# Two layers' query and key block products dealt out in one written order, and a tail with its projection and additions rearranged

## The chip, the cores and the metric

The kernel runs on one core of a Trainium2 chip. The metric is the device time of one execution in microseconds (us); lower is better. The time before is 3595.53 us, the median of three runs (3595.47 to 3596.08). One more execution was recorded by the hardware profiler; its own numbers are in the table below.

A core has five engines that run side by side and wait for each other through semaphores: TensorE (PE; PEld is its loading of weights), VectorE (DVE), ScalarE (ACT), GpSimd (POOL) and SyncE (SP), which mostly issues transfers. Matmul results land in PSUM, in banks of 512 fp32 values per partition, and VectorE or ScalarE take them out.

## The reference, cut to what matters

The input is 16 images of 256 channels and 1024 positions. Each goes through two layers, all in fp32. Both layers compute queries, keys and values from the tokens:

```python
# layer 0, 4 heads of 64
qkv = (xs @ w_proj + b_proj).reshape(B, S, N_HEADS, 3 * D_K)
q, k, v = jnp.split(qkv, 3, axis=-1)
attn = jax.nn.softmax(jnp.einsum('bihd,bjhd->bijh', q, k) * SCALE, axis=2)
res = jnp.einsum('bijh,bjhd->bihd', attn, v).reshape(B, S, N_HEADS * D_K)
x = res @ w_out + b_out + xs
# layer 1, 8 heads of 32
x = x + attention(group_norm(x, gn1_w, gn1_b), qkv_w, proj_w, proj_b, phys_bias)
h = gelu(mlp_w1 @ group_norm(x, gn2_w, gn2_b) + mlp_b1, approximate=False)
out = x + mlp_w2 @ h + mlp_b2
```

The change concerns `q` and `k` of both layers, the order of some sums around them, and, for the last image alone, the projection of layer 1 (`res @ proj_w`) and the additions of the second MLP matmul to the output.

## The kernel before, in words

The images run through a software pipeline. While image b is in attention, pieces of the MLP of image b-1 and of the `v` of image b+1 are put between its steps. For images 1 to 14 (14 times in all) there is a stage between layer 0's attention and layer 1's attention of image b. It holds, on TensorE, the first half of the previous image's MLP (`hidden`, line 1206), then `q` and `k` of layer 0 for image b+1 and of layer 1 for image b (line 1103), then layer 1's scores (line 642).

There `q` and `k` are not made by eight block products for each half of the output channels but by seven. Four blocks of the input (two halves of the channels by two halves of the positions) and four of the weights are combined beforehand: the input sums `t1` to `t4` by four VectorE instructions (`input_sums`, lines 1088 to 1091), the weight sums once, at the beginning. Then `qk_by_seven` issues products p1 to p7 for each of two channel halves `ch`. All products of a half gather in three PSUM banks: two banks of one "wide" tile (`both`), and one bank `y`. Between products, ScalarE copies a state of a bank aside (`qk7p`, lines 1128 to 1136) or out as `k` (lines 1109, 1111), and VectorE takes out `q` (lines 1115, 1117). A later product into the same tile has to wait for such a reader.

In what follows a product is named by layer, number and half: "a20" is product 2 of half 0 for layer 0 (image b+1), "b31" product 3 of half 1 for layer 1 (image b).

What decides the order of the work: the program issues pieces in a written order, but instructions without a marker can be moved by the building layer's scheduler, which gives every engine one fixed order before the run. `keep_in_program_order` takes an instruction out of that freedom, and `issue_after(x)` keeps what stands in its block behind the instruction x. On the chip each engine then works through its own list in order; at the head of a list an instruction waits for its semaphores.

In the kernel before, the products have no marker. The build puts p7 of half 1 of layer 0 (a71) into the MLP's first half, and mixes the others. The layer-1 input sums are made as soon as the group norm's four `gn_g` instructions (line 928) are done. On VectorE they stand ahead of the last GELU sums of the MLP's first half (lines 1262, 1263 and 1282; the first two read MLP products from PSUM, and the third waits for ScalarE's GELU, line 1221). The `v` product of layer 1's first positions comes in the middle of the block products.

The tail belongs to the last image. From the end of its second attention on, a list `nc.in_order` is set, and every instruction of VectorE and TensorE issued through it keeps the written order; such instructions carry the helper's line, L64. The projection `j` of a position half (`out_proj`, `issue`) runs, for each output half, over both input halves; the second input half waits for VectorE's scaling of `res_b`. Six additions of the previous image's MLP result to the output (`add_up`, line 1343, `x<-x,lent`) are held in the list `put_off` together with the sums for a range check, and are all issued within the first pieces of the last image's MLP (`begin`).

Of the kernel before, what the change touches and what calls it, by code (L numbers as in the profile page):

```python
# [283 lines left out]
def first_pass(ctx, tc, x, out, k):  # L284
# [55 lines left out]
    def bank(name, n):  # L340
        return ps_a.tile([P, TB], F32, tag=f"b{n}", name=name)
# [273 lines left out]
    def attention_b(b, qT, kT, v, project):  # L615
# [134 lines left out]
        def normalise(i, r, last):  # L750
            t, c = items[i]
            at_end = last and b == B - 1
            den = bank(f"den_{key}_{i}", 1)
            for g in range(G):
                nc.tensor.matmul(
                    den[g * D : (g + 1) * D, :],
                    k["eones"][:, c * G + g],
                    sums[i][:, g, :],
                    start=True,
                    stop=True,  # L760
                )
            full = work.tile([P, TB], F32, tag="full", name=f"rd_{key}_{i}", bufs=2)
            if at_end:

                held = work.tile([P, TB], F32, tag="full", name="den_held", bufs=2)
                nc.scalar.copy(held, den)
                nc.vector.reciprocal(full, den)
                scale(i, r, last, full)
                put_off.append(lambda: add_to_range(held, full))
                return  # L770
            denominators(
                f"{key}_{i}", den, full, full,
                (3, 5) if last else (1, 1),
                lambda full: scale(i, r, last, full),
            )
# [33 lines left out]
    def out_proj(key, w, src, bias, xs, t, stats, then, late=False):  # L809
        todo = list(range(CC))  # L810

        def issue(cos=range(CC), apart=False):
            home = None if apart else spare.pop("home", None)
            apart = apart or cols[0] == P
            if not apart:
                both = wide(f"{key}_{t}")
            ps = {}

            def leave(co, held=None):
                y = xs[:, co, t * TB : (t + 1) * TB]  # L820
                nc.vector.scalar_tensor_tensor(
                    y, ps[co] if held is None else held[:, co], bias[:, co : co + 1], y,
                    ALU.add, ALU.add,
                )
                nc.vector.bn_stats(stats[:, co, t, :], y)
                if held is None:
                    todo.remove(co)

            def add_up(held):
                with tc.issue_after(spread_out["es"].ins):  # L830
                    for co in range(CC):
                        leave(co, held)

            def part(co, kc):
                product(
                    ps[co],
                    w[:, kc, co * P : (co + 1) * P],
                    src(kc),
                    start=(kc == 0),
                    stop=(kc == CC - 1),  # L840
                )

            for co in cos:
                ps[co] = bank(f"{key}_{t}_{co}", co) if apart else both[:, co, :]
            if apart:
                for co in cos:
                    for kc in range(CC):
                        part(co, kc)
                    leave(co)
            else:  # L850
                for kc in range(CC):
                    for co in cos:
                        part(co, kc)
                if home is not None:
                    held = home[:, 2:4]
                    nc.scalar.copy(held, both)
                    later.after(1, lambda: add_up(held))
                elif late:
                    later.after(2, lambda: [leave(co) for co in cos])
                else:  # L860
                    for co in cos:
                        leave(co)
            if not todo and then:
                then()

        return issue
# [227 lines left out]
    made_k = []  # L1094

    def qk_by_seven(key, block, s, x, q, kk, bias=None):
        ps, got = {}, []

        def half(d, ch, t):
            return d[:, ch, t * TB : (t + 1) * TB]  # L1100

        def mm(to, w, right, first):
            nc.tensor.matmul(  # L1103
                to, w, x[right], start=first, stop=True, skip_group_check=not first
            )

        def leave_k(to, what, ch):
            if bias is None:
                made_k.append(nc.scalar.copy(to, what))
            else:  # L1110
                nc.scalar.activation(to, what, AF.Identity, bias=bias[:, 1, ch : ch + 1])

        def leave_q(to, what, more, ch):
            if bias is None:
                nc.vector.tensor_add(to, more, what)
            else:
                nc.vector.scalar_tensor_tensor(
                    to, what, bias[:, 0, ch : ch + 1], more, ALU.add, ALU.add
                )

        def p1(ch):
            both = wide(f"qk7_{key}_{ch}")
            ps[ch] = both[:, 0, :], both[:, 1, :], bank(f"qk7y_{key}_{ch}", 1 - ch)
            if not got:
                got.append(weights_tile(f"qk7p_{key}"))
            one, two, _ = ps[ch]
            mm(one, block(1, ch, 0), "b11", True)
            nc.scalar.copy(two, one)

        def p7(ch):  # L1130
            mm(ps[ch][2], s[:, ch, 2], "t3", True)
            nc.scalar.copy(got[0][:, 2 * ch], ps[ch][2])

        def p6(ch):
            mm(ps[ch][1], s[:, ch, 1], "t2", False)
            nc.scalar.copy(got[0][:, 2 * ch + 1], ps[ch][1])

        def p2(ch):
            mm(ps[ch][0], block(1, ch, 1), "b21", False)
            leave_k(half(kk, ch, 0), ps[ch][0], ch)  # L1140

        def p4(ch):
            mm(ps[ch][2], block(0, ch, 1), "t4", False)
            leave_q(half(q, ch, 0), ps[ch][2], got[0][:, 2 * ch + 1], ch)

        def p5(ch):
            mm(ps[ch][1], s[:, ch, 0], "t1", False)
            leave_q(half(q, ch, 1), ps[ch][1], got[0][:, 2 * ch], ch)

        def p3(ch):  # L1150
            mm(ps[ch][1], s[:, ch, 3], "b22", False)
            leave_k(half(kk, ch, 1), ps[ch][1], ch)

        return [
            lambda p=p, ch=ch: p(ch)
            for p, ch in (
                (p1, 0), (p1, 1), (p7, 0), (p7, 1), (p6, 0), (p6, 1), (p2, 0),
                (p5, 0), (p5, 1), (p4, 0), (p4, 1), (p2, 1), (p3, 0), (p3, 1),
            )
        ]  # L1160

    inputs = {}

    put_off = []

    def sums_of_input(b, y, part=None):
        extra = act.tile([P, 3, TB], F32, tag="hs", name=f"hs_{b}")
# [26 lines left out]
    def mlp(b, xb):  # L1194
# [30 lines left out]
        def begin(i):  # L1225
# [14 lines left out]

            if not nc.in_order:
                return add_once()
            put_off.insert(i, add_once)
            if i:
                while put_off:
                    put_off.pop(0)()
                nc.in_order.clear()

        def middle(i):
# [6 lines left out]
        def finish(i):  # L1256
# [3 lines left out]
            products_of(i, [(7, ps[:, 0, :], False), (6, ps[:, 1, :], False)])  # L1260
            rest = gs[1, 1, i]
            nc.vector.tensor_add(unit(0, 0, i), rest, ps[:, 0, :])  # L1262
            nc.vector.tensor_add(rest, rest, ps[:, 1, :])
            gelu(0, 0, i, gs[0, 0, i])
            gelu(1, 1, i, rest)
            combine((1, 0), (0, 0), False, i)
# [195 lines left out]
    for b in range(B):  # L1462
        def load_next(b=b):
# [3 lines left out]
            with tc.issue_after(spread_out["last"].ins):  # L1467
                load_blocks(1, b - 1)
                if b + 1 < B:
# [2 lines left out]
        later.after(14, load_next)  # L1472
        xn = []
        seven = 0 < b < B - 1
        sums_1 = {}
        run(
            attention_0(
                b, tiles0, xs[b],
                lambda st, b=b, xn=xn, seven=seven, sums_1=sums_1: group_norm(
                    f"g{b}", xs[b], st, k["g1w"], k["g1b"], "res", xn, 2 if b else 1,  # L1480
                    (lambda y: sums_1.update(input_sums(f"b{b}", y))) if seven else None,
                ),
            )
        )
# [4 lines left out]
        if seven:  # L1489
# [2 lines left out]
            run_pieces(hidden[1:2])  # L1492
            with tc.issue_after(mlp_made["begun"].ins):
                sums_0 = input_sums(f"a{b}", xs[b + 1])
            run_pieces(hidden[2:])
            first = first_v
            run_pieces(
                qk_by_seven(
                    f"a{b}", qk_block_0, qk_parts[:, 0], sums_0, *tiles0[:2], k["bqk"]
                )  # L1500
            )
        else:
            run_pieces(first[:5] if b == 0 else hidden)
        later.flush()
# [7 lines left out]


        if seven:
            made = qk_by_seven(f"b{b}", qk_block_1, qk_parts[:, 1], sums_1, *tiles1[:2])
            run_pieces(made[:4] + v[:1] + made[4:7])
            with tc.issue_after(made_k[-1].ins):
                mlp_made["exp"]()
            run_pieces(made[7:])
        else:  # L1520
            aside.extend((1, 0))
            run_pieces(qk[:n] + v[:1])
# [48 lines left out]
    run_pieces(hidden)  # L1571
    with tc.issue_after(mlp_made["begun"].ins):
        check()
    run_pieces(outputs[:-1] + [lambda part=part: outputs[-1](part, 2) for part in range(2)])

def general_pass(ctx, tc, x, out, k):
# [290 lines left out]
```

## Time and profile before

| what | before |
|---|---|
| median of the runs | 3595.53 us |
| the profiled execution itself | 3596.98 us |
| its span from first to last instruction | 3595.2 us |
| TensorE, VectorE, ScalarE busy | 3581.2, 2785.7, 2286.5 us |
| one block-product stage (301.36 to 327.16 us) | 25.80 us, TensorE busy 25.80 |
| in it VectorE, ScalarE busy | 12.45, 14.76 us |
| TensorE clock granted | 1.00 |

The profile is one execution. A line of its timeline gives the start in us from the span's beginning, the length, the engine, the source line, the operation, output<-inputs by the program's names, the shape, and how many equal instructions in a row are drawn together; in square brackets stands how long the engine was idle before it and what ended that. An fp32 matmul appears as two passes, so one product is "x2". Matmuls overlap: each pass is drawn longer than the time until the next may follow, so TensorE can look fully busy while it waits. In group tables "mean ns" is one instruction's length. "issue" means that the profile shows nothing the engine waited for.

### The profile page before, as it was taken

The numbers are of one execution on the slowest core, as the hardware profiler recorded it, in microseconds if no ns is written. First come the engines' busy times: TensorE is split into PE (matmuls) and PEld (weight loads), VectorE is DVE, ScalarE is ACT, GpSimd is POOL, SyncE is SP. The second block draws the span as 40 slices with busy tenths as digits, with TensorE's granted clock in tenths as the row PEclk, the third lists the DMA queues.
The fourth block names the chain that finished last, engine by engine and source line by source line (L and its number), as shares of the span: only waits on it lengthen the run. The fifth ranks groups of instructions, "written<-read, shape, count | busy, mean of one in ns | idle before, by whom it ended". The sixth has DMA issues, their size and how long they took to land.

```text
span 3595.2 us, 81996 instructions
## 1 busy us (share of the span) xinstructions
PE 3581.2 (100%) x35713; PEld 1470.5 (41%) x35713; DVE 2785.7 (77%) x3188; ACT 2286.5 (64%) x3186; POOL 217.7 (6%) x319
## 2 busy tenths in 40 slices
PE   9999999999999999999999999999999999999999
PEld 4334344343444434444344443434434444344434
DVE  5786877868788687876868878688786877869787
ACT  4665757567575665856658566585765757657573
POOL 4000000000000010000000000000000100000000
PEclk9999999999999999999999999999999999999999
DMA  4011312213122131221312213121121211213100
GB/s 133 8 58 33 84 48 41 71 39 82 45 44 68 39 81 45 52 66 34 81 45 52 66 33 81 45 55 63 38 77 45 55 63 43 72 45 64 52 28 28
DMA packets 81605, 198.06 MB, mean 55 GB/s; under 512 B 38006, under 2 KB 38774, under 8 KB 75094
## 3 DMA queue, kind: packets, MB, share of 16 engines
q1 hardware_dynamic: 71860, 164.13, 15.0%
q0 software_dynamic: 7632, 28.21, 5.1%
q8 instruction: 282, 4.62, 0.5%
q14 instruction: 85, 0.70, 0.1%
q10 hardware_dynamic: 1746, 0.40, 0.1%
HBM read 125.59 MB, written 22.27 MB: 41 GB/s over the span
## 4 chain that ended last, share of the span: by engine, by line
PE 91%; DVE 4%; DMA 2%; issue 1%; SPq 1%; ACT 1%; ACTq 0%; DVEq 0%
PE s_b L642 12%; PE s_a L458 12%; PE acc_a L481 12%; PE acc_b L696 12%; PE m L381 9%; PE m L1206 9%; PE qk_b L1103 4%; PE qk_a L1103 3%; PE v_b L381 3%; PE j L381 3%; PE o L381 3%; PE v_a L381 3%; PE qk7y_b L1103 1%; DVE es_b L670 1%; PE qk7y_a L1103 1%
## 5 line engine op out<-in xcount | busy, mean ns | idle before, releaser
L655 ACT ACTIVATE e_b<-s_b 128x1024 f32<-128x1024 f32 (+1 forms) x1280 | 983.4, 866 | 135.6 <-PE s_b L642 135.6
L670 DVE TENSOR_TENSOR es_b<-es_b,e_b 128x2048 f32<-128x2048 f32 (+1 forms) x460 | 881.8, 1935 | 104.9 <-ACT e_b L655 88.1
L468 ACT ACTIVATE e_a<-s_a 128x1024 f32<-128x1024 f32 x512 | 521.8, 1026 | 358.9 <-PE s_a L458 358.3
L458 PE MATMUL s_a<-q,k 64*64 64x512 f32 x4096 | 544.3, 593 | 0.4 <-DVE res_a L502 0.4
L481 PE MATMUL acc_a<-e_a,v 64*64 64x512 f32 x4096 | 540.2, 589 | 0.0
L642 PE MATMUL s_b<-q,k 32*64 32x512 f32 x8192 | 523.5, 600 | 2.7 <-ACT v L978 1.3
L495 DVE TENSOR_TENSOR es_a<-es_a,e_a 128x1024 f32<-128x1024 f32 x384 | 471.8, 1229 | 62.7 <-ACT e_a L468 42.7
L696 PE MATMUL acc_b<-e_b,v 128*32 128x512 f32 x4096 | 492.1, 598 | 0.0
L381 PE MATMUL m<-g,w 128*32 128x256 f32 (+1 forms) x6432 | 401.8, 384 | 0.0
L381 PEld LDWEIGHTS m<-g,w 128*32 128x32 f32 x6432 | 218.7, 111 | 205.1 <-issue 55.1
L481 PEld LDWEIGHTS acc_a<-e_a,v 64*64 64x64 f32 x4096 | 188.0, 133 | 251.4 <-issue 215.0
L642 PEld LDWEIGHTS s_b<-q,k 32*64 32x64 f32 x8192 | 175.7, 130 | 248.2 <-issue 133.2
L458 PEld LDWEIGHTS s_a<-q,k 64*64 64x64 f32 x4096 | 175.9, 133 | 247.4 <-issue 208.3
L696 PEld LDWEIGHTS acc_b<-e_b,v 128*32 128x32 f32 x4096 | 108.4, 109 | 351.6 <-ACT e_b L655 194.7
L670 DVE TENSOR_TENSOR es_b<-e_b,e_b 128x2048 f32<-128x2048 f32 (+1 forms) x72 | 147.1, 2052 | 131.4 <-ACT e_b L655 131.4
L1206 PE MATMUL m<-gn_h,w 128*128 128x512 f32 x504 | 238.4, 601 | 1.1 <-DVE g L1234 0.7
L1282 DVE TENSOR_TENSOR g<-g,g 128x512 f32<-128x512 f32 (+1 forms) x184 | 193.9, 1064 | 1.2 <-PE m L381 0.7
L1206 PE MATMUL m<-hs,w 128*128 128x512 f32 x380 | 175.8, 592 | 0.0
L1221 ACT ACTIVATE g<-g,m1b 128x512 f32<-128x512 f32 x128 | 91.6, 722 | 113.9 <-DVE g L1262 85.6
L1206 PEld LDWEIGHTS m<-gn_h,w 128*128 128x128 f32 x504 | 91.7, 190 | 114.8 <-issue 98.1
L1221 ACT ACTIVATE g<-m,m1b 128x512 f32<-128x512 f32 x128 | 81.1, 685 | 78.6 <-PE m L1206 78.6
L381 PE MATMUL v_a<-wp,x 128*32 128x256 f32 (+1 forms) x1952 | 121.7, 379 | 0.0
(252 smaller groups left out, 3558.4 us busy)
## 6 DMA issues: line engine op xcount, KB each, us to landing
w<-w_kept SPq DMA_DIRECT2D x30, 1792.0 KB
packed_b<-es_b SPq DMA_DIRECT2D x42, 512.0 KB
packed_b<-es_b POOLq DMA_DIRECT2D x42, 512.0 KB, 6.2
rd_b<-row_b SPq DMA_DIRECT2D x252, 64.0 KB
out_dram<-x SPq DMA_DIRECT2D x63, 256.0 KB
d_a<-row_a SPq DMA_DIRECT2D x62, 256.0 KB
x<-in_x_dram SPq DMA_DIRECT2D x30, 512.0 KB
qk<-qk_kept SPq DMA_DIRECT2D x14, 1024.0 KB
```

The costliest lines, as they stand in the source:

```text
L381: nc.tensor.matmul(o[sl], w[:, sl], r, **flags)
L458: nc.tensor.matmul(s[h : h + HALF, g, :], kT[g * D : (g + 1) * D, c, kb * P + h : kb * P + h + HALF], qT[g * D : (g + 1) * D, c, t * TB : ...
L468: nc.scalar.activation(e, s, AF.Exp, scale=float(D) ** -0.5)
L481: nc.tensor.matmul(accs[i][h][g * D : (g + 1) * D, :], v[h * HALF : (h + 1) * HALF, kb, c * 2 + g], e[h * HALF : (h + 1) * HALF, g, :], st ...
L495: spread_out["es"] = nc.vector.tensor_add(sums[i], held[i] if kb == 1 else sums[i], e)
L642: nc.tensor.matmul(outs[g][h : h + HALF, :], kT[g * D : (g + 1) * D, c, k0 : k0 + HALF], qT[g * D : (g + 1) * D, c, t * TB : (t + 1) * TB] ...
L655: spread_out["exp"] = nc.scalar.activation(to, s, AF.Exp, scale=float(D) ** -0.5)
L670: ins = nc.vector.tensor_add(d, (d if kb else es[0][:, g : g + step]), es[m][:, g : g + step])
L696: nc.tensor.matmul(acc[g * D : (g + 1) * D, :], v[:, kb + m, c * G + g], es[m][:, g, :], start=(m == 0), stop=(m == 1),)
L1103: nc.tensor.matmul(to, w, x[right], start=first, stop=True, skip_group_check=not first)
L1206: nc.tensor.matmul(ps, blocks[1][number - 1][:, i * P : (i + 1) * P], inputs[b][number], start=first, stop=True, skip_group_check=not first,)
L1282: (nc.vector.tensor_add if plus else nc.vector.tensor_sub)(d, d, more)
```

## The change

In the stage between the attentions, the layer-0 and layer-1 products are given one written order, and every product but a71 is kept in it. The wide tile of layer 0's half 0 is chosen by hand (the second in the rotation). The bank `y` of a half is now taken when its p7 is issued, not at p1. a71 is written into the MLP's first half. The layer-1 input sums are issued behind the last sum of the MLP's first half (`made["added"]`, the second addition in `finish`). The `v` product comes last but one, before b31.

In the tail, the projection runs over the input half outside and the output half inside, into a wide tile instead of two single banks. The list is split in two: `checked` holds the sums of the range check and the additions of open MLP sums, still issued in `begin`; `put_off` holds the additions to the output, now issued after `check()`, behind the last `begin`.

```diff
-                put_off.append(lambda: add_to_range(held, full))
+                checked.append(lambda: add_to_range(held, full))
...
-            if apart:
+            if apart and not nc.in_order:
                 for co in cos:
                     for kc in range(CC):
                         part(co, kc)
...
-            nc.tensor.matmul(
+            ins = nc.tensor.matmul(
                 to, w, x[right], start=first, stop=True, skip_group_check=not first
             )
+            if ps:
+                tc.keep_in_program_order(ins)
...
         def p1(ch):
-            both = wide(f"qk7_{key}_{ch}")
-            ps[ch] = both[:, 0, :], both[:, 1, :], bank(f"qk7y_{key}_{ch}", 1 - ch)
+            both = wide(f"qk7_{key}_{ch}", order[1] if ch == 0 and bias is not None else None)
+            one, two = ps[ch] = both[:, 0, :], both[:, 1, :]
             mm(one, block(1, ch, 0), "b11", True)
             nc.scalar.copy(two, one)
 
         def p7(ch):
-            mm(ps[ch][2], s[:, ch, 2], "t3", True)
-            nc.scalar.copy(got[0][:, 2 * ch], ps[ch][2])
+            ys[ch] = bank(f"qk7y_{key}_{ch}", 1 - ch)
+            mm(ys[ch], s[:, ch, 2], "t3", True)
+            nc.scalar.copy(aside_for()[:, 2 * ch], ys[ch])
...
-            put_off.insert(i, add_once)
+            checked.insert(i, add_once)
             if i:
-                while put_off:
-                    put_off.pop(0)()
+                for fn in checked:
+                    fn()
                 nc.in_order.clear()
...
-            nc.vector.tensor_add(rest, rest, ps[:, 1, :])
+            made["added"] = nc.vector.tensor_add(rest, rest, ps[:, 1, :])
...
-            run_pieces(hidden[2:])
+            made = {"a": qk_by_seven(
+                f"a{b}", qk_block_0, qk_parts[:, 0], sums_0, *tiles0[:2], k["bqk"]
+            )}
+            run_pieces(hidden[2:8] + [made["a"][7, 1]] + hidden[8:])
             first = first_v
-            run_pieces(
-                qk_by_seven(
-                    f"a{b}", qk_block_0, qk_parts[:, 0], sums_0, *tiles0[:2], k["bqk"]
-                )
-            )
...
-            made = qk_by_seven(f"b{b}", qk_block_1, qk_parts[:, 1], sums_1, *tiles1[:2])
-            run_pieces(made[:4] + v[:1] + made[4:7])
+            with tc.issue_after(mlp_made["added"].ins):
+                sums_1 = input_sums(f"b{b}", xn_made[0])
+            made["b"] = qk_by_seven(
+                f"b{b}", qk_block_1, qk_parts[:, 1], sums_1, *tiles1[:2]
+            )
...
+            run_pieces(pieces(
+                "a10 a70 a11 a60 a40 a61 a50 a41 a51 a20 b10 a21 a30 b60 a31 b11 b70"
+                " b50 b61 b71 b20"
+            ))
             with tc.issue_after(made_k[-1].ins):
                 mlp_made["exp"]()
-            run_pieces(made[7:])
+            run_pieces(pieces("b51 b40 b30 b21 b41") + v[:1] + pieces("b31"))
...
     with tc.issue_after(mlp_made["begun"].ins):
         check()
+        for fn in put_off:
+            fn()
```

More of the change, by code (lines that the diff above doesn't have):

```diff
@@ L1096, in qk_by_seven, with aside_for @@
     def qk_by_seven(key, block, s, x, q, kk, bias=None):
-        ps, got = {}, []
+        ps, ys, got = {}, {}, []
+        def aside_for():
+            if not got:
+                got.append(weights_tile(f"qk7p_{key}"))
+            return got[0]
         def half(d, ch, t):
@@ L1121, in p1 @@
         def p1(ch):
-            both = wide(f"qk7_{key}_{ch}")
-            ps[ch] = both[:, 0, :], both[:, 1, :], bank(f"qk7y_{key}_{ch}", 1 - ch)
-            if not got:
-                got.append(weights_tile(f"qk7p_{key}"))
-            one, two, _ = ps[ch]
+            both = wide(f"qk7_{key}_{ch}", order[1] if ch == 0 and bias is not None else None)
+            one, two = ps[ch] = both[:, 0, :], both[:, 1, :]
             mm(one, block(1, ch, 0), "b11", True)
@@ L1130, in p7 @@
         def p7(ch):
-            mm(ps[ch][2], s[:, ch, 2], "t3", True)
-            nc.scalar.copy(got[0][:, 2 * ch], ps[ch][2])
+            ys[ch] = bank(f"qk7y_{key}_{ch}", 1 - ch)
+            mm(ys[ch], s[:, ch, 2], "t3", True)
+            nc.scalar.copy(aside_for()[:, 2 * ch], ys[ch])
         def p6(ch):
             mm(ps[ch][1], s[:, ch, 1], "t2", False)
-            nc.scalar.copy(got[0][:, 2 * ch + 1], ps[ch][1])
+            nc.scalar.copy(aside_for()[:, 2 * ch + 1], ps[ch][1])
         def p2(ch):
@@ L1142, in p4 @@
         def p4(ch):
-            mm(ps[ch][2], block(0, ch, 1), "t4", False)
-            leave_q(half(q, ch, 0), ps[ch][2], got[0][:, 2 * ch + 1], ch)
+            mm(ys[ch], block(0, ch, 1), "t4", False)
+            leave_q(half(q, ch, 0), ys[ch], got[0][:, 2 * ch + 1], ch)
         def p5(ch):
@@ L1152, in p3 @@
             leave_k(half(kk, ch, 1), ps[ch][1], ch)
[L1154 to L1158, printed above, removed]
-            )
-        ]
+        return {
+            (n, ch): lambda p=p, ch=ch: p(ch)
+            for n, p in ((1, p1), (2, p2), (3, p3), (4, p4), (5, p5), (6, p6), (7, p7))
+            for ch in range(CC)
+        }
     inputs = {}
-    put_off = []
+    put_off, checked = [], []
     def sums_of_input(b, y, part=None):
@@ L1474, in first_pass @@
         seven = 0 < b < B - 1
-        sums_1 = {}
+        xn_made = []
         run(
@@ L1478, in first_pass @@
                 b, tiles0, xs[b],
-                lambda st, b=b, xn=xn, seven=seven, sums_1=sums_1: group_norm(
+                lambda st, b=b, xn=xn, seven=seven, xn_made=xn_made: group_norm(
                     f"g{b}", xs[b], st, k["g1w"], k["g1b"], "res", xn, 2 if b else 1,
-                    (lambda y: sums_1.update(input_sums(f"b{b}", y))) if seven else None,
+                    xn_made.append if seven else None,
                 ),
@@ L1494, in first_pass @@
                 sums_0 = input_sums(f"a{b}", xs[b + 1])
-            run_pieces(hidden[2:])
+            made = {"a": qk_by_seven(
+                f"a{b}", qk_block_0, qk_parts[:, 0], sums_0, *tiles0[:2], k["bqk"]
+            )}
+            run_pieces(hidden[2:8] + [made["a"][7, 1]] + hidden[8:])
             first = first_v
-            run_pieces(
-                qk_by_seven(
-                    f"a{b}", qk_block_0, qk_parts[:, 0], sums_0, *tiles0[:2], k["bqk"]
-                )
-            )
         else:
@@ L1514, in first_pass, with pieces @@
         if seven:
-            made = qk_by_seven(f"b{b}", qk_block_1, qk_parts[:, 1], sums_1, *tiles1[:2])
-            run_pieces(made[:4] + v[:1] + made[4:7])
+            with tc.issue_after(mlp_made["added"].ins):
[3 more added lines that the diff above has]
+            )
+            def pieces(names):
+                return [made[n[0]][int(n[1]), int(n[2])] for n in names.split()]
+            run_pieces(pieces(
+                "a10 a70 a11 a60 a40 a61 a50 a41 a51 a20 b10 a21 a30 b60 a31 b11 b70"
+                " b50 b61 b71 b20"
+            ))
             with tc.issue_after(made_k[-1].ins):
                 mlp_made["exp"]()
-            run_pieces(made[7:])
+            run_pieces(pieces("b51 b40 b30 b21 b41") + v[:1] + pieces("b31"))
         else:
```

## The prediction

> **What bounds the kernel now.** I read the page's busy shares first, then the chain that ended last:
>
> ```profile
> PE 3581.2 (100%) x35713; PEld 1470.5 (41%) x35713; DVE 2785.7 (77%) x3188; ACT 2286.5 (64%) x3186; POOL 217.7 (6%) x319
> PE 91%; DVE 4%; DMA 2%; issue 1%; SPq 1%; ACT 1%; ACTq 0%; DVEq 0%
> ```
>
> TensorE is never free, so with an unchanged set of matmuls only waits inside its stream can go. They do not show as idle time: a matmul that waits is drawn longer. So I read the timeline of TensorE in one block-product stage (301.36 to 327.16 us, 25.80 us long; all 14 such stages have this length):
>
> ```profile
> 301.36 1.02 PE L1103 MATMUL qk_a<-x,wp 128*128 128x512 f32 x2
> ...
> 303.93 1.11 PE L1103 MATMUL qk_a<-x,wp 128*128 128x512 f32 x2
> ...
> 308.31 1.11 PE L1103 MATMUL qk_a<-x,wp 128*128 128x512 f32 x2
> 309.25 1.02 PE L1103 MATMUL qk_b<-gn_g,wq 128*128 128x512 f32 x2
> 310.20 1.13 PE L1103 MATMUL qk_a<-qk7t_a,qk 128*128 128x512 f32 x2
> ...
> 312.88 1.88 PE L1103 MATMUL qk_a<-x,qk 128*128 128x512 f32 x4
> 314.68 1.12 PE L1103 MATMUL qk_b<-gn_g,wq 128*128 128x512 f32 x2
> ...
> 319.94 1.11 PE L1103 MATMUL qk_b<-gn_g,wq 128*128 128x512 f32 x2
> 320.88 1.96 PE L1103 MATMUL qk_b<-qk7t_b,qk 128*128 128x512 f32 x4
> ...
> 325.26 1.97 PE L1103 MATMUL qk_b<-gn_g,qk 128*128 128x512 f32 x4
> ```
>
> A product is two passes; a clean one shows 1.02 us and gives way after 0.858 (301.36 to 302.21), two show 1.88. The surplus is the wait: 0.09 (303.93), 0.09 (308.31), 0.19 (310.20: it starts 0.95 after 309.25 instead of 0.86, and is 0.11 too long), 0.19 (314.68, likewise), 0.09, 0.08 and 0.09: together 0.81 us a stage, 11.3 us in 14.
>
> The price of a lateness comes from 310.20: ScalarE's `k` copy ends at 310.14, the weight load starts at 310.19, and the matmul streams as if from 310.30. So a product starts no earlier than release + 0.05 + 0.105 us; a release up to 0.70 us after the preceding product's start is free.
>
> VectorE at the same place, then its pace where each instruction needs the one before:
>
> ```profile
> 299.72 0.54 DVE L928 TENSOR_SCALAR gn_g<-x,rstd_g,gma_g 128x512 f32<-128x512 f32 x1
> 300.17 0.69 DVE L1089 TENSOR_TENSOR qk7t_b<-gn_g 128x512 f32<-128x512 f32 x1
> 300.77 0.69 DVE L1088 TENSOR_TENSOR qk7t_b<-gn_g 128x512 f32<-128x512 f32 x1
> ...
> 308.94 0.74 DVE L1117 SCALAR_TENSOR_TENSOR q<-qk_a,bqk,qk7p_a 128x512 f32<-128x512 f32 x1
> ...
> 947.97 0.69 DVE L1090 TENSOR_TENSOR qk7t_a<-x,qk7t_a 128x512 f32<-128x512 f32 x1
> 948.69 0.69 DVE L1091 TENSOR_TENSOR qk7t_a<-x,qk7t_a 128x512 f32<-128x512 f32 x1
> ```
>
> It is full from 299.7 to 309.7: 0.60 us an instruction, 0.72 in a dependent pair. In the tail (helper line L64):
>
> ```profile
> 3527.35 2.84 PE L64 MATMUL j<-res_b,wpj 128*128 128x512 f32 x6 [0.32 <-DVE res_b L64]
> 3533.32 0.33 PEld L64 LDWEIGHTS gm_h<-mean_c_h,gavg 128*128 128x128 f32 x2 [0.52 <-DVE mean_c_h L64]
> 3548.90 2.49 DVE L64 TENSOR_TENSOR x<-x,lent 128x512 f32<-128x512 f32 x4
> 3553.85 1.98 PE L1206 MATMUL m<-gn_h,w 128*128 128x512 f32 x4
> 3556.25 2.84 PE L1206 MATMUL m<-gn_h,w 128*128 128x512 f32 x6 [0.42 <-DVE g L1263]
> ```
>
> The projection `j` loses 0.59 us. The additions at 3548.90, with two at 3551.90, stand ahead of the GELU sums that 3553.85 and 3556.25 wait for: 0.28 + 0.68 = 0.97 us.
>
> **What the Trainium skill says.** "TensorE: Matmul & The Clock Gate", Step-by-step: weight loads are pulled ahead of running matmuls, matmuls stay in order. The trace agrees: 0.19 us loads cost nothing until their release is late. "Perfetto Trace Analysis", Identifying the Most-Contended Engine: matmul busy time misjudges headroom because matmuls are pipelined; here 100% busy contains the 0.81. "VectorE: DVE Perf Modes", The TRN2 errata: an fp32 add of N takes (N+151)/0.96 ns, 691 for 512; the trace has 0.69.
>
> **The change, part by part.** The built orders of both kernels hold the same instructions on every engine (17,861 matmuls); SP's and POOL's orders are identical, so no DMA moves.
>
> *New product order.* I replayed the order by hand with these durations, time 0 at the stage's first product (a10); the next should each come 0.858 later. Between two users of one bank there now always stand at least two other products, so the second's turn is 2.57 after the first. The first's result can be read from 1.06 (1.02 and 0.04 to pass on); a copy of 0.58 to 0.69 ends by 1.75, and with 0.155 the next can go at 1.91: 0.67 to spare. This holds where the reading engine is free, as for all of layer 1; the six waits from 308.31 on, 0.72, go by it. The first, 0.09, goes because a11's bank is freed by L1266 at 0.23, 1.3 before it is needed.
>
> *The layer-1 sums now stand behind the GELU sums.* VectorE's new order from the fourth `gn_g` (at -1.64): L1265 -1.18; L1266 -0.46 (dependent, 0.72); L1285 0.32 (L1265 ends -0.50, GELU 0.72 with 0.10 of hand-overs); then at 0.60 each L1265 0.92, L1285 1.52, L1266 2.12, L1285 2.72, L1088 3.32, L1285 3.92, L1089 4.52; the eviction of a40 5.12 (0.75 long); L1090 5.78; L1091 6.51 (dependent); the eviction of a50 7.11 to 7.86. a20 uses the other half of a50's two-bank tile and, in the built order, waits for that eviction. Its turn is 9 x 0.858 = 7.72; it can go at 7.86 + 0.155 = 8.02. So a new wait of 0.30 us arises; b10 and every product behind it, and their copies, move with it. The next, a21, needs the eviction of a51 (8.43 to 9.18, so 9.34) at 10.03: free. a61 needs ScalarE's copy for a11 (3.47 to 4.05, behind a GELU): 4.21 against 4.29, free by 0.08 only.
>
> *Moves that I cost at nothing.* The copy for a71 (0.58) goes to a ScalarE gap of 2.64 us before 295.3. The `v` product (8 matmuls of 0.216) keeps its length; its VectorE copy (0.69) now ends 0.7 before its bank is asked for; without that cover it would cost up to 0.69. The exp table load (1.28) stands between two `k` copies that begin 2.57 apart, with 0.4 to spare. No edit touches the first scores: the last `k` copy stands before them as now.
>
> Per stage: 0.81 - 0.30 = 0.51 us; times 14: 7.1 us.
>
> *Tail.* With the input half outermost, a second j product (0.86) runs before the one that waited, covering 0.59. But the wait turns up next at gm_h: its load was released at 3533.32 by the VectorE chain, which does not move, and can stream at 3533.42 against 3533.46 now. Gain 0.04. Additions later: 0.97 goes; by the dependent pair behind `hs` about 0.06 is left: gain 0.91. The six additions (3.6 us) fall in the VectorE gap of 3.26 us before 3564.28; the 0.2 that hangs over meets over 1 us of room at the next user.
>
> Sum: 7.1 + 0.95 = 8.05 us. On the profiled execution (3596.98, span 3595.2) that is a span of 3587.1; the median, 3595.53, lies 1.45 below that execution and gives 3587.5.
>
> **Rivals.**
> 1. *No new wait.* VectorE reaches a50's eviction 0.3 us sooner (if the dependent pairs overlap as independent ones do, 0.24 of it). Saved 11.3 + 0.95: 3583.3. Against: 947.97 to 948.69 shows 0.72.
> 2. *VectorE one instruction later.* A GELU on ScalarE, now mixed with copies, misses its turn: 0.60 more, wait 0.90, stage 0.09 longer: 3595.5 + 1.3 - 0.95 = 3595.9, no change. For: a61 and the L1285s have little room; against: each GELU as replayed ends 0.3 before its L1285.
> 3. *Slower.* The same queue before a50's eviction, two instructions late (1.2 us): wait 1.5, (1.5 - 0.81) x 14 - 0.95 = +8.7: 3604.2. The sign turns where the eviction ends 0.58 us later than 7.86. Against: VectorE's whole queue ends at 309.7 now with the same instructions.
> 4. *The tail gives nothing*, if the additions delay the last GELU sums instead: 3588.4.
>
> **How the numbers follow.** Forecast 0.60 (with its own range 3586.1 to 3589.6, for a wait of 0.20 to 0.45), rival 1 0.16, rival 2 (and what lies between) 0.16, rival 3 0.04, rival 4 0.04. What this kernel's measurement can tell from no change is 0.2%, 7.2 us; the forecast lies just beyond, and its waits over 0.36 fall short: about a sixth of it. Faster: 0.50 + 0.16 + 0.01 = 0.67; same: 0.10 + 0.16 + 0.03 = 0.29; slower 0.04. The range runs from a little below rival 1 to halfway to rival 2: 3582.5 to 3592; it leaves out most of rival 3 and the worse part of 2.
>
> **What would show it.** The 14 stages should take 25.3 us; in them only a20 (`qk_a<-x,wp`, ten products in) longer than 1.02 us or started late, released by VectorE's `q<-qk_a`. gm_h in the tail should start late, 3556.25's wait be gone. A stage of 25.0 speaks for rival 1; 25.8 or more, with waits for VectorE, for 2 or 3. The prediction is wrong if attention after the stage lengthens, or if further products wait.

## The result, and the profile after

The changed kernel takes 3587.72 us (median; 3586.34 to 3588.80), the kernel before in the same comparison 3595.77 us: 8.05 us less, a ratio of 0.9977 with a 95% interval of 0.9969 to 0.9986. The forecast was 3587.5. The interval, 0.14 to 0.31% less, is clear of no change; the 0.2% that the prediction names as what the measurement can tell lies inside it. The execution that was profiled took 3587.91 us, with a span of 3586.1.

The page's busy shares of the changed kernel:

```profile
PE 3573.3 (100%) x35713; PEld 1479.0 (41%) x35713; DVE 2785.1 (78%) x3188; ACT 2288.7 (64%) x3186; POOL 220.1 (6%) x319
```

The instructions are the same in number, and VectorE and ScalarE are as busy as before. TensorE's busy time fell by 7.9 us of the 9.1 by which the two profiled spans differ, although it does the same matmuls: most of what was saved had been drawn as work.

The timeline of TensorE in the same stage, now 301.28 to 326.55 us, 25.27 us long (the other 13: 25.26 or 25.27):

```profile
301.28 1.02 PE L1108 MATMUL qk_a<-x,wp 128*128 128x512 f32 x2
...
303.00 1.02 PE L1108 MATMUL qk_a<-x,wp 128*128 128x512 f32 x2
...
305.57 1.88 PE L1108 MATMUL qk_a<-qk7t_a,qk 128*128 128x512 f32 x4
...
308.15 1.02 PE L1108 MATMUL qk_a<-qk7t_a,qk 128*128 128x512 f32 x2
309.17 1.13 PE L1108 MATMUL qk_a<-x,wp 128*128 128x512 f32 x2
310.13 1.02 PE L1108 MATMUL qk_b<-gn_g,wq 128*128 128x512 f32 x2
...
323.87 1.89 PE L381 MATMUL v_b<-wq,gn_g 128*128 128x256 f32 x8
325.59 1.02 PE L1108 MATMUL qk_b<-gn_g,qk 128*128 128x512 f32 x2
326.55 1.97 PE L642 MATMUL s_b<-q,k 32*64 32x512 f32 x32
```

Every product is clean (1.02, or 1.88 for two) but one: a20, at 309.17, starts 1.02 instead of 0.86 after a51 and is 0.11 too long. That is a wait of 0.27 us. a61 and a50 (305.57) run on without a gap. The timeline of the weight loads names what released it:

```profile
308.15 0.19 PEld L1108 LDWEIGHTS qk_a<-qk7t_a,qk 128*128 128x128 f32 x1 [0.24 <-issue]
309.17 0.30 PEld L1108 LDWEIGHTS qk_a<-x,wp 128*128 128x128 f32 x2 [0.83 <-DVE q L1124]
```

Other loads are idle for 0.24 us, a20's for 0.83, until VectorE's `q`. VectorE before it (its lines with `q` are evictions: it takes a finished product out of PSUM):

```profile
300.10 0.68 DVE L1265 TENSOR_TENSOR g<-g,m 128x512 f32<-128x512 f32 x1
300.81 0.69 DVE L1266 TENSOR_TENSOR g<-g,m 128x512 f32<-128x512 f32 x1
...
307.05 0.68 DVE L1090 TENSOR_TENSOR qk7t_b<-gn_g,qk7t_b 128x512 f32<-128x512 f32 x1
307.76 0.69 DVE L1091 TENSOR_TENSOR qk7t_b<-gn_g,qk7t_b 128x512 f32<-128x512 f32 x1
308.37 0.75 DVE L1124 SCALAR_TENSOR_TENSOR q<-qk_a,bqk,qk7p_a 128x512 f32<-128x512 f32 x1
```

The eviction of a50 runs from 7.09 to 7.84 us after the stage's start; both dependent pairs are 0.71 apart. The tail:

```profile
3517.80 3.60 PE L64 MATMUL j<-res_b,wpj 128*128 128x512 f32 x8
...
3525.12 0.38 PE L64 MATMUL gm_h<-mean_c_h,gavg 128*128 128x2 f32 x2 [0.29 <-DVE mean_c_h L64]
...
3544.57 1.93 PE L1209 MATMUL m<-gn_h,w 128*128 128x512 f32 x4
...
3547.20 2.74 PE L1209 MATMUL m<-gn_h,w 128*128 128x512 f32 x6
```

`j` runs through, `gm_h` waits in its place, and of the two waits for the GELU sums 0.05 us is left (1.93 instead of 1.88).

| part of the trace | before | after |
|---|---|---|
| 14 block-product stages, sum | 361.20 | 353.66 |
| tail, from the last image's last scores to the last matmul | 76.31 | 75.36 |
| 14 attentions behind the stages, sum | 1442.75 | 1442.07 |

The stages gave 7.54 us, the tail 0.95. The 0.68 in the attentions comes up again below.

### The profile page after: what moved, and what is told of

Read it like the earlier page. It is cut to its first block, busy times and chain, and to the rows that moved or that the text cites. A ratio compares the mean times of both kernels' runs of the same rounds, so it can differ in the third digit from the quotient of the medians.

```text
span 3586.1 us, 82054 instructions
## 1 busy us (share of the span) xinstructions
PE 3573.3 (100%) x35713; PEld 1479.0 (41%) x35713; DVE 2785.1 (78%) x3188; ACT 2288.7 (64%) x3186; POOL 220.1 (6%) x319
## 4 chain that ended last, share of the span: by engine, by line
PE 93%; DVE 4%; DMA 1%; issue 1%; SPq 0%; ACT 0%; DVEq 0%
PE s_b L642 13%; PE s_a L458 13%; PE acc_a L481 12%; PE acc_b L696 12%; PE m L1209 9%; PE m L381 9%; PE qk_a L1108 3%; PE qk_b L1108 3%; PE v_b L381 3%; PE j L381 3%; PE v_a L381 3%; PE o L381 3%; PE qk7y_b L1108 1%; PE qk7y_a L1108 1%; DVE es_b L670 1%
## 5 line engine op out<-in xcount | busy, mean ns | idle before, releaser
L1122 DVE TENSOR_TENSOR q<-qk7p_b,qk_b 128x512 f32<-128x512 f32 x28 | 19.3, 688 | 134.5 <-PE qk_b L1108 134.5
```

## Experiments

"Stage" is the length from a10 to the first scores; 25.80 before and 25.26 in the changed kernel. All ratios are to the kernel before.

### 1. The stage alone, the tail alone

The changed kernel with the tail of before:

```diff
-            if apart and not nc.in_order:
+            if apart:
...
-                for fn in checked:
-                    fn()
+                while put_off:
+                    put_off.pop(0)()
...
-        for fn in put_off:
-            fn()
```

> The changed stage, with the tail as before. My theory: all of 0.54 us a stage (25.80 to 25.26 us, 14 stages) comes from here, and the 0.66 us by which the attentions behind the stages were shorter in the changed kernel goes with it: 7.5 + 0.7 = 8.2 us less than the kernel before, about 3587.4. In the tail the waits of m for the GELU sums (3553.85, 3556.25 before) are back. Rival (the tail gives more than it shows): under 6 us.

Measured: 3588.78 us, ratio 0.9979 (0.9971 to 0.9988); stages 25.26 us, tail 76.29. In this comparison the kernel before takes 3596.23 us, so the gain is 7.45 us, not 8.2.

Then the kernel before with both edits of the tail:

> The kernel before with the two edits of the tail alone. My theory: the stages stay at 25.80 us, the tail ends 0.95 us sooner, time about 3594.7 against 3595.7; gm_h waits for mean_c_h, about 0.3 us. Rival (the additions, put behind the GELU sums, delay something later in the tail): no gain, or a tail over 0.3 us longer than in the changed kernel.

Measured: 3595.98 us, ratio 1.0000 (0.9991 to 1.0009); stages 25.79, tail 75.35 us. One microsecond is less than the runs resolve; the trace resolves it. So the stage gives nearly everything, and the two parts don't touch each other. What fell is my guess that the shorter attentions belong to the stage. With the stage as before, the attentions that nothing disturbs take 102.83 us here, exactly as in the changed kernel; in the trace of the kernel before they take 102.87.

### 2. The tail's two edits apart

Only the projection by input half (`if apart and not nc.in_order:` in the kernel before):

> The kernel before with the projection j by input half alone. My theory: j loses its wait of 0.59 us but gm_h, released by a VectorE chain that doesn't move, starts as late as before: the tail (from the last scores s_b to the last matmul) is 76.27 us against 76.31. Rival (the wait was on the path): 75.7.

Measured in one profiled execution: the tail is 76.27 us. Its timeline:

```profile
3525.38 3.60 PE L64 MATMUL j<-res_b,wpj 128*128 128x512 f32 x8
3532.69 0.38 PE L64 MATMUL gm_h<-mean_c_h,gavg 128*128 128x2 f32 x2 [0.28 <-DVE mean_c_h L64]
...
3553.18 1.98 PE L1206 MATMUL m<-gn_h,w 128*128 128x512 f32 x4
3555.58 2.84 PE L1206 MATMUL m<-gn_h,w 128*128 128x512 f32 x6 [0.42 <-DVE g L1263]
```

The wait has only moved to `gm_h`. Then only the additions later (the list split in two, as in the diff of the change):

> The kernel before with the additions to the output later, and j as before. My theory: the waits of the m products at 3553.85 and 3556.25 go but for 0.05 us; the tail is 75.4 us against 76.31 before and 75.36 with both edits; j still waits 0.5 us. Rival (the two edits need each other): 76 us or more.

Measured likewise: the tail is 75.38 us, with the wait in `j` still there and 0.05 us left at `m`:

```profile
3525.46 2.84 PE L64 MATMUL j<-res_b,wpj 128*128 128x512 f32 x6 [0.32 <-DVE res_b L64]
...
3550.93 1.93 PE L1206 MATMUL m<-gn_h,w 128*128 128x512 f32 x4
```

So the two edits give 0.04 and 0.92 us.

### 3. The order without the place of the sums, and the place without the order

The changed kernel with the layer-1 sums back ahead of the GELU sums:

```diff
-                    xn_made.append if seven else None,
+                    (lambda y: xn_made.append(input_sums(f"b{b}", y))) if seven else None,
...
-            with tc.issue_after(mlp_made["added"].ins):
-                sums_1 = input_sums(f"b{b}", xn_made[0])
+            sums_1 = xn_made[0]
```

> The changed kernel with the layer-1 input sums at their old place, ahead of the last GELU sums on VectorE. My theory: the new order begins with a11 as third product, whose bank is freed by the last GELU sum (line 1266); with four sums ahead of it that sum comes about 2.3 us later, so a11 waits about 1.0 us; the wait of a20 for the eviction of a50 is then gone, since VectorE's queue behind is the shorter. Stage 25.9 to 26.0 us, so all of the stage's gain is lost: time 3595 to 3597. Rival (the written order is what gives, the place of the sums is a detail): stage 25.0 to 25.3, time under 3588.

Measured: 3597.69 us, ratio 1.0003 (0.9994 to 1.0012), just above the forecast range; stages 25.94 us, as forecast. TensorE's timeline there:

```profile
302.21 1.02 PE L1108 MATMUL qk7y_a<-qk7t_a,qk 128*128 128x512 f32 x2
303.91 1.13 PE L1108 MATMUL qk_a<-x,wp 128*128 128x512 f32 x2 [0.68 <-DVE g L1266]
...
309.17 1.02 PE L1108 MATMUL qk_a<-qk7t_a,qk 128*128 128x512 f32 x2
310.02 1.02 PE L1108 MATMUL qk_a<-x,wp 128*128 128x512 f32 x2
```

a11 (303.91) waits for L1266, which gives back its bank, and a20 (310.02) no longer waits. a11 starts 1.70 instead of 0.86 us after its predecessor and is 0.11 too long: a wait of 0.95 us. Without it the stage would be 25.0; this one wait takes the whole gain of the stage.

The kernel before with the sums late and its own order of products:

```diff
...
+            with tc.issue_after(mlp_made["added"].ins):
+                sums_1 = input_sums(f"b{b}", xn_made[0])
             made = qk_by_seven(f"b{b}", qk_block_1, qk_parts[:, 1], sums_1, *tiles1[:2])
```

> The kernel before with the layer-1 input sums issued behind the last GELU sums, and nothing else of the change. My theory: the scheduler's own order for the products comes with waits of 0.19 and 0.39 us for ScalarE's copies, since ScalarE and VectorE are late together at the stage's beginning; stage 25.9 to 26.1 us and up to 0.45 us at its beginning, so 2 to 8 us slower than before. Rival (the place of the sums is what gives, the written order is a detail): stage under 25.5 us, time under 3591.

Measured: 3602.14 us, 5.9 us slower than before, ratio 1.0017 (1.0010 to 1.0023); stages 25.95 us, and the stretch ahead of them, from the end of layer 0's attention to a10, 33.58 instead of 33.31 in most cases: (0.15 + 0.27) x 14 = 5.9. Two of the waits in the stage show in pairs of products drawn as 2.07 instead of 1.88 us, 0.19 each:

```profile
307.06 2.07 PE L1103 MATMUL qk_a<-qk7t_a,qk 128*128 128x512 f32 x4
...
311.54 2.07 PE L1103 MATMUL qk_a<-x,qk 128*128 128x512 f32 x4
```

So neither edit gains alone. With the order alone a11 waits for a GELU sum; with the late sums alone products wait at other places. With both, none of these waits is left.

### 4. The wait that the change left

The changed kernel with one VectorE instruction, the last layer-1 sum, moved behind the eviction of a50:

```diff
-        nc.vector.tensor_sub(t4, b21, t2)
+        later_t4.append(lambda: nc.vector.tensor_sub(t4, b21, t2))
...
-            run_pieces(pieces(
-                "a10 a70 a11 a60 a40 a61 a50 a41 a51 a20 b10 a21 a30 b60 a31 b11 b70"
+            def last_sum():
+                with tc.issue_after(made_q[-1].ins):
+                    late.pop()()
+
+            run_pieces(pieces("a10 a70 a11 a60 a40 a61 a50") + [last_sum] + pieces(
+                "a41 a51 a20 b10 a21 a30 b60 a31 b11 b70"
...
```

> The changed kernel with one VectorE instruction moved: the last of the layer-1 sums (t4, line 1091) behind the eviction of a50. My theory: a20 waits only because VectorE's queue reaches that eviction late; 0.72 us of queue less and it ends at 7.1 instead of 7.84 us after the stage's start, before a20 needs it (7.57). The wait of 0.27 us goes and nothing takes its place: stage 24.98 to 25.0 us, 14 x 0.27 = 3.8 us less than the changed kernel, about 3584 against 3587.7. Rival (a wait that takes the place of the one removed: a51's eviction, a21, or ScalarE's copy for a61, free by 0.08 us only): stage 25.1 to 25.3, gain under 2 us.

Measured: 3584.79 us, ratio 0.9967 (0.9955 to 0.9979); stages 25.00 us. VectorE and TensorE there (L1127 evicts, L1094 is the moved sum):

```profile
307.13 0.74 DVE L1127 SCALAR_TENSOR_TENSOR q<-qk_a,bqk,qk7p_a 128x512 f32<-128x512 f32 x1
307.79 0.68 DVE L1094 TENSOR_TENSOR qk7t_b<-gn_g,qk7t_b 128x512 f32<-128x512 f32 x1
```

```profile
307.64 1.02 PE L1111 MATMUL qk_a<-qk7t_a,qk 128*128 128x512 f32 x2
308.50 1.02 PE L1111 MATMUL qk_a<-x,wp 128*128 128x512 f32 x2
```

The eviction is over at 307.87 and a20 starts at 308.50, 0.86 after a51: no wait, and none takes its place.

The same from TensorE's side, VectorE's queue unchanged:

```diff
-                "a10 a70 a11 a60 a40 a61 a50 a41 a51 a20 b10 a21 a30 b60 a31 b11 b70"
-                " b50 b61 b71 b20"
+                "a10 a70 a11 a60 a40 a61 a50 a41 a51 b10 a20 a21 b60 a30 a31 b70"
+                " b11 b50 b71 b61 b20"
...
-            run_pieces(pieces("b51 b40 b30 b21 b41") + v[:1] + pieces("b31"))
+            run_pieces(pieces("b40 b51 b41 b30 b21") + v[:1] + pieces("b31"))
```

> The changed kernel with another order of the products from a20 on: b10 before a20, and then a20 a21 b60 a30 a31 b70 b11 b50 b71 b61 b20, b40 b51 b41 b30 b21, v, b31, so that two other products stand between all users of one bank again. VectorE's queue is as in the changed kernel. My theory: a20's turn comes 0.86 us later (8.58), after the eviction is done (7.84 + 0.16), so the wait is covered: stage 24.98 to 25.0 us, about 3584, as with the last sum moved. Rival (a21, now 0.86 us behind a20 and waiting for the eviction of a51, 0.66 us behind that of a50, waits instead: free by 0.05 us only): stage 25.05 to 25.3.

Measured: 3583.96 us, ratio 0.9964 (0.9951 to 0.9978); stages 25.00 us.

```profile
309.04 1.02 PE L1108 MATMUL qk_b<-gn_g,wq 128*128 128x512 f32 x2
309.90 1.88 PE L1108 MATMUL qk_a<-x,wp 128*128 128x512 f32 x4
```

a20 and a21 (309.90) follow b10 without a wait. Both versions beat both kernels: by the traces 14 x 0.26 = 3.7 us below the changed kernel, and their slowest run (3585.29) is faster than its fastest (3586.34). Their stages are equally long; what lies between the two medians, 0.83 us, does not come from there (see the last section).

Only a20 and b10 exchanged ("a51 b10 a20 a21 a30 b60 ..."):

> The changed kernel with a20 and b10 exchanged and nothing else. My theory: a20's wait of 0.27 us goes, but now a30 comes with one product (a21) between it and a20, whose k copy by ScalarE it needs; as in the kernel before that costs 0.19 us. Stage 25.26 - 0.27 + 0.19 = 25.18 us, 1 us less than the changed kernel: 3586 to 3587. Rival (one product between is enough): stage 25.0, 3584.

Measured: 3587.05 us, ratio 0.9974 (0.9963 to 0.9984); stages 25.18 us. The timeline shows the new wait, at a30 (312.09), with a20 and a21 at 310.29 just ahead:

```profile
310.29 1.88 PE L1108 MATMUL qk_a<-x,wp 128*128 128x512 f32 x4
312.09 1.12 PE L1108 MATMUL qk_a<-x,qk 128*128 128x512 f32 x2
```

It starts 1.80 instead of 1.72 after a20 and is 0.10 too long: 0.19 us, the price that the kernel before paid at the same kind of place (310.20 there). One product between two users of a tile is not enough. The bank isn't the unit here: a20 goes into the first bank of the tile, and its `k` copy reads that one, while a30 goes into the second bank. a30 waits all the same, as a20 does in the changed kernel for the eviction of a50's bank. So these are waits for a tile of two banks. Whether they would go with the two banks as separate tiles was not tried.

### 5. One VectorE instruction more

The changed kernel with the first layer-1 sum written a second time, with the same values:

```diff
                 sums_1 = input_sums(f"b{b}", xn_made[0])
+                y = xn_made[0]
+                nc.vector.tensor_sub(sums_1["t3"], y[:, 1, TB:], y[:, 0, TB:])
```

> The changed kernel with one more VectorE instruction among the layer-1 sums (t3 written a second time with the same values). It stands ahead of the eviction of a50. My theory: all that VectorE is later goes into a20's wait. The instruction takes 0.60 us, of which 0.12 comes back if the dependent pair L1090, L1091 is no longer back to back: wait 0.75 to 0.87 us, stage 25.74 to 25.86 us, 6.7 to 8.4 us more than the changed kernel, 3594 to 3596. Rival (VectorE has room there, or the products behind take the delay up): stage under 25.5, time under 3591.

Measured: 3594.88 us, ratio 0.9995 (0.9986 to 1.0003), which does not tell it apart from the kernel before. The medians are 1.8 us apart, and the trace gives the same: 14 x 0.06 in the stages, which take 25.74 us, and 0.95 in the tail.

```profile
306.97 0.68 DVE L1090 TENSOR_TENSOR qk7t_b<-gn_g,qk7t_b 128x512 f32<-128x512 f32 x1
307.57 0.74 DVE L1124 SCALAR_TENSOR_TENSOR q<-qk7y_a,bqk,qk7p_a 128x512 f32<-128x512 f32 x1
308.23 0.68 DVE L1091 TENSOR_TENSOR qk7t_b<-gn_g,qk7t_b 128x512 f32<-128x512 f32 x1
308.83 0.74 DVE L1124 SCALAR_TENSOR_TENSOR q<-qk_a,bqk,qk7p_a 128x512 f32<-128x512 f32 x1
```

a20 waits 0.75 us. The eviction of a40 now stands between the dependent L1090 and L1091, so the queue grows by 0.48, not 0.60, and all of it shows in the stage: 25.74 - 25.26 = 0.48. Nothing behind takes the delay up.

### 6. The `v` product in the middle

```diff
-                "a10 a70 a11 a60 a40 a61 a50 a41 a51 a20 b10 a21 a30 b60 a31 b11 b70"
-                " b50 b61 b71 b20"
+                "a10 a70 a11 a60 a40 a61 a50 a41 a51 a20 b10 a21 a30") + v[:1] + pieces(
+                "b60 a31 b11 b70 b50 b61 b71 b20"
...
-            run_pieces(pieces("b51 b40 b30 b21 b41") + v[:1] + pieces("b31"))
+            run_pieces(pieces("b51 b40 b30 b21 b41 b31"))
```

> The changed kernel with the v product of layer 1 in the middle of the block products (behind a30, so 13 products in) instead of last but one. My theory: while block products run, four halves share three wide tiles; v as a further user there takes a tile that is not free before ScalarE's k copy of a30, which has just started, and b11 then gets its tile later too: two waits of about 1.04 us, and 0.09 at b31. Stage 25.26 + 2.1 = 27.4 us, about 30 us more than the changed kernel, 3617. Rival (the v product is neutral wherever it stands, only its length counts): 25.3, 3588.

Measured: 3618.39 us, ratio 1.0062 (1.0046 to 1.0079); stages 27.44 us. TensorE's timeline there:

```profile
313.55 1.99 PE L381 MATMUL v_b<-wq,gn_g 128*128 128x256 f32 x8 [0.78 <-ACT k L1118]
...
318.04 1.12 PE L1108 MATMUL qk_b<-gn_g,wq 128*128 128x512 f32 x2 [0.78 <-ACT k L1118]
```

`v` waits for a tile that a30's `k` copy still holds, and b11 then in the same way for the `k` copy of a31. Here `v` isn't neutral; where the change puts it, it is.

## Why the prediction was right, point by point

- **The 0.81 us of old waits goes.** Shown: none of the seven places is left, and with the new wait removed the stage is 25.00 us (25.80 - 0.81 = 24.99). That the first of them needed the sums out of the way is shown by the early sums.
- **Two products between users of a bank suffice, one doesn't.** Shown by the exchange of a20 and b10: 0.19 us. The prediction's own sum gives this size: the second user can go 1.91 us after the first, and one product between gives it its turn after 1.72. But "bank" should read "tile", as the prediction itself takes it for a20 ("the other half of a50's two-bank tile").
- **A new wait of a20 for the eviction of a50.** Right in place and cause. Forecast 7.11 to 7.86 after the stage's start, measured 7.09 to 7.84; so 0.27 us, not 0.30. The last sum later and the other order remove it from either side.
- **Moves costed at nothing.** a61, free by only 0.08, held. So did `v`. Neither the copy for a71 nor the exp table load shows a wait behind it; these two had no run of their own. Nor had the tile chosen by hand and the later taking of the bank `y`: they were measured only together with the written order.
- **Sum of the stages.** 7.1 forecast, 7.54 in the trace: 14 x 0.54. The missing 0.03 a stage is the smaller wait.
- **Tail.** Forecast 0.04 and 0.91, measured alone 0.04 and 0.92, together 0.95. The wait in `j` did turn up at `gm_h`.
- **Total.** 8.05 forecast and 8.05 between the medians. This agreement to the hundredth is chance: the spans differ by 9.1, 8.5 from stages and tail, the rest from the attentions.
- **Rivals.** The first (no new wait) would have given 3583.3; it is what the two better versions do (3584.8 and 3584.0, 11.9 and 12.7 us below the kernel before in their comparison; the rival says 12.2). The second (one instruction late) was sized at 3595.9 with a wait of 0.90; as an experiment it gave a wait of 0.75 and 3594.9, because the additional instruction breaks up a dependent pair (0.12 of the difference) and the wait it adds to was 0.27, not 0.30. That VectorE can fall behind because of a late GELU, as this rival has it, no run tried. For the third, with a turn at 0.58 us, there is one point: 0.48 later leaves 1.8 us of gain, where 14 x (0.58 - 0.48) = 1.4 would be left by the forecast's slope.

## What to carry to other kernels

When several products accumulate by turns in few PSUM tiles, write the order so that from the start of one user of a tile to the start of the next at least as much time passes as matmul, copy and hand-over take together. Here that is 1.06 + 0.69 + 0.155 = 1.91 us; two products between give 2.57, one gives 1.72 and costs 0.19. Then replay the reading engine's queue in order: the wait that remains is where that queue comes last. An instruction whose result is needed late should not stand ahead of an eviction; moving one sum of 0.69 us was worth 0.26 us in every stage. Test an order and the queue of the engine that empties its banks together, since here each alone gave nothing or lost.

## What was not expected of the hardware

Stretches that no edit touches differ between the traces, of which there is one for each kernel. Of the 14 attentions behind the stages, 4 to 8 stand out by up to 0.9 us (103.7 instead of 102.8); the second, the eighth and the thirteenth do in every trace, each time by another amount. In the second one of the kernel before, the scaling of `res_b` waits for a transfer of the denominators, and `j` for the scaling:

```profile
640.03 0.69 DVE L779 TENSOR_TENSOR res_b<-res_b,rd_b 128x512 f32<-128x512 f32 x1 [3.07 <-DMA rd_b<-row_b]
```

```profile
640.78 1.92 PE L381 MATMUL j<-res_b,wpj 128*32 128x512 f32 x16 [0.63 <-DVE res_b L779]
```

In an undisturbed attention of the same trace the scaling waits 1.71 us and `j` not at all. Over all thirteen traces the sum of the 14 varies from 1441.4 to 1443.1 us: with 0.7 us between the two kernels, nothing there can be put down to the change. Why the landing varies stays open.

The undisturbed attentions, in turn, have one length within a trace: 102.87 us in the kernel before, 102.78 in the version with the other order from a20 on, 102.83 in the other eleven. Such a step comes 14 times, 0.6 to 0.7 us in all: most of the 0.68 between the two kernels, and most of what separates the two better versions. Its cause, and whether it comes back when the same kernel runs again, stays open too.
